# Attention residual: x plus the output's bias made in DRAM by accumulating DMAs instead of on GpSimd

## The chip, the cores and the metric

The kernel runs on one core of a Trainium2 chip. The metric is the device time of one execution in microseconds (us). The core has five engines that run their own instruction streams in order: TensorE (PE, matrix products; PEld is its weight load), VectorE (DVE), ScalarE (ACT), GpSimd (POOL) and SyncE (SP, which here only issues DMAs). 16 DMA engines move data between DRAM and the on-chip memory; SP, ACT and POOL each have a queue into them.

## The reference, cut to what matters

Four sequences of 1024 tokens, 512 channels, 16 heads of 32. First a cross attention on a layernorm of x, with a mask by token groups (768 image tokens in three chunks that see only their own chunk, then 256 text tokens that see all image tokens and, causally, text), then a feed-forward block with fake-quantised activations and weights. All of it is float32.

```python
def _L0_xattn_ref(q, kv, Wq, bq, Wk, bk, Wv, bv, Wo, bo, txt_tok_len, img_tok_len):
    ...
    attn = jax.nn.softmax(scores, axis=-1)
    out = jnp.einsum('bhqk,bhkd->bhqd', attn, vh)
    out = out.transpose(0, 2, 1, 3).reshape(B, N, C)
    return out @ Wo + bo

x = x + _L0_xattn_ref(_layernorm(x, axis=-1), ctx_1024, ...)
x = x + _L0_ffn_ref(_layernorm(x, axis=-1), ...)
```

The sum `x + out @ Wo + bo` is what the change is about. The kernel folds the bias of the values into it as well: since the softmax rows sum to one, `bv @ Wo + bo` is one row of 512 numbers that is added to every token. It is called the output's bias below.

## The kernel before, in words

**Blocks and units.** The 4096 tokens are cut into 16 query blocks of 256 tokens, numbered c = 0 to 15, four to a sequence: three image blocks and one text block. A unit is one block, one group of four heads (g = 0 to 3) and, for text, one block of keys (part 0 to 3). There are 112 units: for a sequence 12 of image blocks, then 16 of the text block (the last sequence has its text block second). Index n of the main loop counts units. In turn n the loop makes the scores of unit n (`s`, L446 or L457), their row maxima on DVE (L450, L468), the shifted scores and exponentials of unit n - 5 (`t` L504 and L509, `pT` L514 and L518) and the product with the values of unit n - 6 (`av` L554). The denominators are sums of the exponentials, made on POOL (`sp` L535) and folded by a product with ones (`av` L573); DVE takes the reciprocal (L588) and POOL multiplies (L589).

**What fills PE between them.** In each turn `large` takes one larger step: a part of the projection of a query, key or value block (`pp_q`, `pp_kv`, `pv`) or of the output projection of a finished block (`po`); all of these are recorded under L226. Jobs come in the order kv 0, q 0, kv 1, q 1 and so on, and a planner (`target`, `can_big`, `can_small`) sets in which turn each step falls. This plan depends on the indices alone, never on times.

**Layernorm of x.** For a coming query block, `next_queries` loads x into the tile `xb` (one buffer, L136 in `load_block`) and puts three functions into the queue `background`: `statistics` (DVE, L365), `deviation` (two ACT and seven small POOL instructions, L370 to L379: layernorm's factors) and `apply` (ACT L383, then the DMA `xn_d<-xb` of SP, L385, which frees `xb`). One function is taken from `background` in each turn; stages of the feed-forward weights' quantisation stand in the same queue. `load_spread` (L146) loads a kv block, or reads `xn_d` back, in the order that VectorE's 32x32 transposes need; `small_step` does that transpose (L267), one turn later at the earliest. In its turn the DVE instructions stand in a fixed order.

**The output of a block.** `Output.load` loads x for the block into `xr` (two buffers). `Output.add_bias` adds the output's bias `bo_b` on POOL (L613, one instruction of 128x1024 for a block), put off to a later turn by the list `later`. `Output.take` adds the product `po` to `xr` on DVE (L618), puts statistics for the second layernorm into `background`, and at the end stores the block into the DRAM tile `x1_d` by a DMA of POOL (L631). The feed-forward stage reads `x1_d` by L1019.

**The output's bias** is made in turns 2 to 5 by `spread`, `product` and `total` (DVE L206 writes `bo_b`).

**Order.** PE, DVE, ACT and POOL run in the order in which the program is written. SP's DMAs are put in order by the framework's scheduler, which moves a DMA forward to where its inputs and its buffer are ready: in the profile the first two `xr` loads are issued at 12.9 and 20.6 us though their blocks end much later. On the chip SP then issues in that fixed order and waits at each for what it needs.

Of the kernel before, what the change touches and what calls it, by code (L numbers as in the profile page):

```python
# [10 lines left out]
F32 = mybir.dt.float32  # L11
# [3 lines left out]
ALU = mybir.AluOpType  # L15
# [4 lines left out]
P = 128  # L20
B, N, C = 4, 1024, 512
NH, D = 16, 32
FF = 1408
NCC = C // P
NIC = FF // P
QB = 256
NQB = N // QB
# [15 lines left out]
def kernel(ctx: ExitStack, tc: tile.TileContext, x, kv, Wq, bq, Wk, bk, Wv, bv, Wo, bo, clip_x, clip_down, w_gate, w_up, w_down, out):  # L43
    nc = tc.nc
    x_tok = x.rearrange("b n c -> (b n) c")
# [5 lines left out]
    dram = ctx.enter_context(tc.tile_pool(name="dram", bufs=1, space=DRAM))  # L51

    x1_d = dram.tile([B * N, C], F32, tag="x1_d", name="x1_d")
    xn_d = [dram.tile([QB, C], F32, tag=f"xn_d{c}", name=f"xn_d{c}") for c in range(B * NQB)]
    h_d = [dram.tile([P, NIC, TB], F32, tag=f"h_d{i}", name=f"h_d{i}") for i in range(NTB - RESIDENT)]

# [65 lines left out]
    with ExitStack() as actx:  # L122
        wk2 = actx.enter_context(tc.tile_pool(name="wk2", bufs=2))
# [4 lines left out]
        ap = actx.enter_context(tc.tile_pool(name="ap", bufs=1))  # L128
# [5 lines left out]
        def load_block(src, c, tag, bufs=1):  # L134
            t = ld.tile([P, 2, C], F32, tag=tag, name=f"{tag}_{c}", bufs=bufs)
            nc.sync.dma_start(t, src[c * QB : (c + 1) * QB, :].rearrange("(t p) c -> p t c", p=P))  # L136
            return t
# [10 lines left out]

        brow = ap.tile([3 * NCC, P], F32, tag="brow", name="brow")
        bqk = ap.tile([P, 3 * NCC], F32, tag="bqk", name="bqk")  # L150
        bo_b = ap.tile([P, C], F32, tag="bo_b", name="bo_b")
        mask = ap.tile([P, P], F32, tag="mask", name="mask")
        NMB = 4
        nm2s = [ap.tile([P, 2, 4, D], BF16, tag=f"nm2_{i}", name=f"nm2_{i}") for i in range(NMB)]
# [18 lines left out]

        def other_loads():
            nc.sync.dma_start(W["Wo"], Wo.rearrange("(c p) f -> p c f", p=P))
            nc.gpsimd.dma_start(bo_b, bo.partition_broadcast(P))
            for name, clip in (("x", clip_x), ("h", clip_down)):
                sig[name] = cpool.tile([P, 1], F32, tag=f"sig_{name}", name=f"sig_{name}")
                nc.gpsimd.dma_start(sig[name], clip.partition_broadcast(P))
# [8 lines left out]
        def output_bias():  # L188

            bvr = wk2.tile([P, NCC, D], F32, tag="wst", name="bvr", bufs=1)  # L190
            parts = wk2.tile([P, C], F32, tag="sp", name="bo_parts")

            def spread():
                nc.vector.memset(bvr, 0.0)
                nc.vector.tensor_copy(bvr[:, :, 0:1], bqk[:, 2 * NCC :].unsqueeze(2))

            def product():
                pb = ps_sc.tile([P, 2, 2, QB], F32, tag="sc", name="pbo").rearrange("p a b c -> p a (b c)")[:, 0, :]
                for cc in range(NCC):
                    nc.tensor.matmul(pb[rows_of(cc)], bvr[:, cc, :], W["Wo"][:, cc, :], start=True, stop=True, tile_position=(0, cc * D), skip_group_check=True)  # L200
                nc.scalar.copy(parts, pb)

            def total():
                pb = ps_sc.tile([P, 2, 2, QB], F32, tag="sc", name="pbt").rearrange("p a b c -> p a (b c)")[:, 0, :]
                nc.tensor.matmul(pb, ones, parts, start=True, stop=True)
                nc.vector.tensor_tensor(bo_b, pb, bo_b, ALU.add)  # L206

            return spread, product, total

# [41 lines left out]
        class Job:  # L251


            def __init__(self, kind, c, a):
                self.kind, self.c, self.a = kind, c, a
                self.small, self.big, self.part = 0, 0, 0
                self.smalls = 2 if c == 0 else 1
                self.bigs = 4 if kind == "kv" else 2
# [93 lines left out]
        background = deque()  # L352
# [54 lines left out]
        def rows_of(j):  # L407
            return slice(j * D, (j + 1) * D)
# [181 lines left out]

                return avs, av, quotient

        at_end = [False]
        later = []

        class Output:


            def __init__(self, k):
                self.k, self.xr, self.i, self.part, self.biased = k, None, 0, 0, False  # L600

            def load(self):
                if self.xr is None:
                    self.xr = load_block(x_tok, self.k.c, "xr", bufs=2)
                    if at_end[0]:
                        later.append(self.add_bias)
                    else:
                        later.append(lambda: later.append(self.add_bias))

            def add_bias(self):  # L610
                if not self.biased:
                    self.biased = True
                    nc.gpsimd.tensor_tensor(self.xr, self.xr, bo_b.unsqueeze(1).to_broadcast([P, 2, C]), ALU.add)  # L613

            def take(self, po, i, cols):
                self.add_bias()
                xr, t0 = self.xr, 2 * self.k.c
                nc.vector.tensor_tensor(xr[:, i, cols], po[:, cols], xr[:, i, cols], ALU.add)  # L618
                if cols.stop < C:
                    return None  # L620
                name = f"st2_{self.k.n}_{i}"

                def statistics():
                    st = small.tile([P, 6], F32, tag="st2", name=name)
                    nc.vector.bn_stats(st, xr[:, i, :])
                    nc.vector.bn_aggr(mv2[:, t0 + i, :], st)
                    nc.vector.tensor_reduce(xm2[:, t0 + i, 0:1], xr[:, i, :], AX.X, ALU.max)
                    nc.vector.tensor_reduce(xm2[:, t0 + i, 1:2], xr[:, i, :], AX.X, ALU.min)

                if i == 1:  # L630
                    nc.gpsimd.dma_start(x1_d[t0 * P : (t0 + 2) * P, :].rearrange("(t p) c -> p t c", p=P), xr)  # L631
                return statistics
# [50 lines left out]
        T_LAG, V_LAG = 5, 6  # L683
        units = []
        for b in range(B):
            for qb in range(NQB) if b < B - 1 else (0, TEXT, 1, 2):
                k = Block(b, qb)
# [3 lines left out]
        LATE = len(units) - n_text - 3 * NCC  # L691
# [94 lines left out]
        def step_output(half=False, rests=False):  # L786
            rest = outputs[0].step(half)
            if outputs[0].i == 2:
                outputs.pop(0)

                def take():
                    rest[1]()
                    for o in outputs[:2]:
                        o.load()

                finish((rest[0], take), rests)
            else:
                finish(rest, rests)
# [57 lines left out]
        stage()  # L856
        stage()
        take()
        spent, rows_done["k", 0] = 2 * BIG, NCC
        stage()  # L860
# [9 lines left out]
        send(3)  # L870
        big_step()
        other_loads()
        early[0] = False
        spread, product, total = output_bias()
        for n in range(len(units) + V_LAG):
            at_end[0] = n >= len(units)
            previous = units[n - 1] if 0 < n <= len(units) else None
            if n < len(units):
                u = units[n]
# [6 lines left out]
                    minus_maxima(u)  # L886
            if n in (2, 3, 4, 5):
                (spread, sigmoids, product, total)[n - 2]()
            f = background.popleft() if background and n > 0 else None
            if f is not None and f.__name__ in ("deviation", "apply", "quantise"):  # L890
                f()
                f = background.popleft() if background and f.__name__ == "quantise" else None
# [100 lines left out]
        for i in range(2):  # L993
            t = t0 + i
# [27 lines left out]
    gctx = ExitStack()  # L1022
    f4 = gctx.enter_context(tc.tile_pool(name="f4", bufs=NTT))
    fd = gctx.enter_context(tc.tile_pool(name="fd", bufs=1))
    fd.tile([P, 56], F32, tag="pad", name="pad")

    fx = gctx.enter_context(tc.tile_pool(name="fx", bufs=2))
    xt = load_x1(fx, 0)
# [160 lines left out]
    def steps(h):  # L1189

        return h.rearrange("p i t -> p (i t)").bitcast(BF16).rearrange("p (i u) -> p i u", i=NIC)[:, :, :TB]
# [9 lines left out]
    for n, tb in enumerate(order):  # L1201
        hq, xr = steps(resident[tb]), xrs.pop(tb)
# [74 lines left out]
```

## Time and profile before

| | |
|---|---|
| time, median of 3 runs | 1131.82 us (1130.69 to 1134.02) |
| the profiled execution | 1132.25 us, span 1130.5 us |
| TensorE clock granted | 0.995 of full speed |
| PE busy | 1106.8 us, 98% of the span |
| DVE, ACT, POOL busy | 783.8, 502.1, 549.0 us |
| POOL L613 (the bias) | 16 instructions, 38.1 us |
| POOL L535 (the sums) | 143 instructions, 328.4 us |
| DMA moved | 119.09 MB, mean 105 GB/s |

The attention stage lasts to about 872 us, the feed-forward stage from there. Idle time of PE in the profile is time between the modelled end of one product and the start of the next; PEld's idle time is the gap in the weight loads, of which some 0.3 us stand at many changes of operation without a loss.

### The profile page before, as it was taken

The numbers are of one execution on the slowest core, as the hardware profiler recorded it, in microseconds if no ns is written. First come the engines' busy times: TensorE is split into PE (matmuls) and PEld (weight loads), VectorE is DVE, ScalarE is ACT, GpSimd is POOL, SyncE is SP. The second block draws the span as 40 slices with busy tenths as digits, with TensorE's granted clock in tenths as the row PEclk, the third lists the DMA queues.
The fourth block names the chain that finished last, engine by engine and source line by source line (L and its number), as shares of the span: only waits on it lengthen the run. The fifth ranks groups of instructions, "written<-read, shape, count | busy, mean of one in ns | idle before, by whom it ended". The sixth has DMA issues, their size and how long they took to land.

```text
span 1130.5 us, 31464 instructions
## 1 busy us (share of the span) xinstructions
PE 1106.8 (98%) x13829; PEld 553.5 (49%) x13851; DVE 783.8 (69%) x980; ACT 502.1 (44%) x701; POOL 549.0 (49%) x616
## 2 busy tenths in 40 slices
PE   9999999999999999999999999999999899998998
PEld 5545545454445445454544445555544344443444
DVE  2546676766577857567777656876666788877887
ACT  3234444343444434344433345544342465553553
POOL 1224556677754576775646668668753232110110
PEclk9999999999999999999999999999999899999999
DMA  8342223132322231331323123112221599311895
GB/s 261 111 132 65 63 56 96 47 97 76 90 63 76 74 97 43 94 104 36 89 66 88 41 74 86 42 50 63 73 76 47 185 289 253 73 34 33 299 379 191
DMA packets 117201, 119.09 MB, mean 105 GB/s; under 512 B 55548, under 2 KB 86536, under 8 KB 115656
## 3 DMA queue, kind: packets, MB, share of 16 engines
q1 hardware_dynamic: 111104, 83.26, 26.7%
q0 software_dynamic: 5648, 33.30, 7.8%
q8 instruction: 108, 1.77, 0.7%
q10 hardware_dynamic: 312, 0.53, 0.2%
q14 instruction: 29, 0.24, 0.1%
HBM read 71.57 MB, written 33.29 MB: 93 GB/s over the span
## 4 chain that ended last, share of the span: by engine, by line
PE 84%; POOL 7%; DVE 3%; DMA 3%; ACT 2%; issue 1%; POOLq 0%; DVEq 0%; SPq 0%; ACTq 0%
PE pv L226 9%; PE pp_kv L226 8%; PE pp_q L226 8%; PE av L554 8%; PE po L226 8%; PE t L509 7%; PE pg L1117 7%; PE pu L1117 7%; PE s L457 5%; POOL sp L535 4%; PE s L446 4%; PE av L573 3%; PE t L504 3%; PE pd L1220 2%; DMA xt<-x_d 2%
## 5 line engine op out<-in xcount | busy, mean ns | idle before, releaser
L514 ACT ACTIVATE pT<-t 128x1024 f32<-128x1024 f32 x112 | 114.8, 1025 | 332.1 <-PE t L509 310.0
L535 POOL TENSOR_TENSOR sp<-sp,pT 128x1024 f32<-128x1024 f32 x84 | 188.2, 2240 | 45.0 <-ACT pT L518 41.6
L535 POOL TENSOR_TENSOR sp<-pT 128x1024 f32<-128x1024 f32 x59 | 140.2, 2376 | 97.7 <-ACT pT L518 86.7
L468 DVE TENSOR_REDUCE nmh<-s 128x2 f32<-128x1024 f32 (+1 forms) x128 | 145.2, 1157 | 60.1 <-PE s L457 57.9
L450 DVE TENSOR_REDUCE nmh<-s 128x4 f32<-128x1024 f32 x96 | 112.8, 1218 | 84.3 <-PE s L446 84.3
L226 PE MATMUL pv<-Wv_sb,kvT 128*32 128x512 f32 (+1 forms) x1088 | 120.5, 570 | 1.6 <-DVE xr L618 1.6
L226 PE MATMUL pp_q<-qT,Wq_sb 128*32 128x256 f32 x2048 | 121.3, 380 | 0.2
L554 PE MATMUL av<-pT,va 128*32 128x256 f32 (+1 forms) x1792 | 116.9, 377 | 0.0
L226 PE MATMUL po<-Wo_sb,oT 128*32 128x512 f32 (+1 forms) x1120 | 112.2, 534 | 2.7 <-DVE xr L618 2.4
L518 ACT ACTIVATE pT<-t 128x1024 f32<-128x1024 f32 x112 | 114.5, 1023 | 0.0
L509 PE MATMUL t<-qT,kT 32*128 32x256 f32 (+1 forms) x1792 | 113.4, 366 | 0.0
L226 PE MATMUL pp_kv<-kvT,Wk_sb 128*32 128x256 f32 x1920 | 112.5, 380 | 0.1
L588 DVE RECIPROCAL avs<-avs 128x256 f32<-128x256 f32 x63 | 109.7, 1742 | 0.0
L509 PEld LDWEIGHTS t<-qT,kT 32*128 32x128 f32 x1792 | 88.1, 184 | 6.7
L1117 PE MATMUL pg<-xqT,wgT 128*128 128x512 bf16 x344 | 90.0, 381 | 1.1 <-DVE xqT L1078 0.5
L1117 PE MATMUL pu<-xqT,wuT 128*128 128x512 bf16 x345 | 90.2, 382 | 0.4
L589 POOL TENSOR_TENSOR oT<-avs 128x256 f32<-128x256 f32 x63 | 46.2, 734 | 90.1 <-DVE avs L588 89.9
L1123 ACT ACTIVATE silu<-pg,sg 128x512 f32<-128x512 f32 x88 | 60.0, 687 | 65.3 <-PE pg L1117 63.2
L226 PEld LDWEIGHTS pp_q<-qT,Wq_sb 128*32 128x32 f32 x2048 | 63.3, 110 | 48.3 <-issue 5.5
L1144 DVE SCALAR_TENSOR_TENSOR h<-pu,su,silu 128x512 f32<-128x512 f32 x88 | 65.4, 747 | 30.5 <-PE pu L1117 27.8
L226 PEld LDWEIGHTS pp_kv<-kvT,Wk_sb 128*32 128x32 f32 x1920 | 60.2, 110 | 43.6 <-issue 2.3
L554 PEld LDWEIGHTS av<-pT,va 128*32 128x32 f32 x1792 | 47.0, 109 | 53.5 <-issue 30.0
(191 smaller groups left out, 1448.0 us busy)
## 6 DMA issues: line engine op xcount, KB each, us to landing
xt<-x_d SPq DMA_DIRECT2D x16, 1024.0 KB, 6.1
h<-h_d POOLq DMA_DIRECT2D x3, 2816.0 KB, 14.2
xb<-in_x_dram SPq DMA_DIRECT2D x16, 512.0 KB, 3.7
xr<-in_x_dram SPq DMA_DIRECT2D x16, 512.0 KB, 3.6
x_d<-xr POOLq DMA_DIRECT2D x16, 512.0 KB, 3.7
spread_kv<-in_ctx_dram SPq DMA_DIRECT2D x60, 128.0 KB, 2.8
xn_d<-xb SPq DMA_DIRECT2D x15, 512.0 KB, 3.4
spread_q<-xn_d SPq DMA_DIRECT2D x60, 128.0 KB, 2.7
```

The costliest lines, as they stand in the source:

```text
L226: nc.tensor.matmul(out[rows_of(j)], lhs[:, rows_of(j)], rhs, start=start, stop=stop, tile_position=(0, j * D), skip_group_check=True)
L450: nc.vector.tensor_reduce(nmh[:, h, :, :, 0], prs[h], AX.X, ALU.max, negate=True)
L468: nc.vector.tensor_reduce(nmh[:, h, :, i, half], s[:, :, :n], AX.X, ALU.max, negate=True)
L509: nc.tensor.matmul(prs[j // 2][:, j % 2, n, cols], kc[rows_of(j), g, n * P : (n + 1) * P], q[rows_of(j), g, cols], start=False, stop=(n == 1))
L514: nc.scalar.activation(pT[:, :2], prs[0], AF.Exp)
L518: nc.scalar.activation(pT[:, 2:], prs[1], AF.Exp)
L535: nc.gpsimd.tensor_tensor(sp[:, :, cols], a, pT[:, :, n, cols], ALU.add)
L554: nc.tensor.matmul(av[rows_of(j), 0, cols], va[:, n, g * P + j * D : g * P + (j + 1) * D], u.pT[:, j, n, cols], start=(u.part == 0 and n = ...
L588: nc.vector.reciprocal(avs[:, 1, :], avs[:, 1, :])
L1117: nc.tensor.matmul(ps, w[:, cc, ic * P : (ic + 1) * P], qT[:, cc, :], start=(cc == 0), stop=(cc == NCC - 1))
L1123: nc.scalar.activation(s, pg, AF.Silu, scale=sg[:, ic : ic + 1])
L1144: nc.vector.scalar_tensor_tensor(h[:, ic, :], pu, su[:, ic : ic + 1], s, ALU.mult, ALU.mult)
```

## The change

Five things are changed.

1. After `total`, SP writes the row `bo_b[:1]` into a DRAM tile `bo_d`, and four DMAs of SP (one for a sequence, 2 MB each) fill all of `x1_d` with copies of that row.
2. In turns n = 7 to 22 a DMA of POOL adds x of block c = n - 7 to those rows of `x1_d` (`accum_op=ALU.add`, DRAM to DRAM, rows of 2 KB).
3. `Output.load` reads `x1_d` instead of x; `add_bias` and its POOL instruction are gone. `xr` has three buffers instead of two.
4. In turns up to LATE in which the exponentials are those of a text unit of part 2 or 3, nothing is taken from `background` if `deviation` is next in it.
5. `bo_b` takes one of the three `oT` buffers instead of its own, and is loaded by SP instead of POOL; a pad in the feed-forward stage grows by 2 KB.

```diff
+    bo_d = dram.tile([1, C], F32, tag="bo_d", name="bo_d")
...
-        bo_b = ap.tile([P, C], F32, tag="bo_b", name="bo_b")
+        bo_b = wk2.tile([P, NCC, QB], F32, tag="oT", name="bo_b", bufs=3).rearrange("p a b -> p (a b)")[:, :C]
...
-            nc.gpsimd.dma_start(bo_b, bo.partition_broadcast(P))
+            nc.sync.dma_start(bo_b, bo.partition_broadcast(P))
...
                 nc.vector.tensor_tensor(bo_b, pb, bo_b, ALU.add)
+                nc.sync.dma_start(bo_d, bo_b[:1, :])
+                for b in range(B):
+                    nc.sync.dma_start(x1_d[b * N : (b + 1) * N, :], bo_d.to_broadcast([N, C]))
...
             def load(self):
                 if self.xr is None:
-                    self.xr = load_block(x_tok, self.k.c, "xr", bufs=2)
-                    if at_end[0]:
-                        later.append(self.add_bias)
-                    else:
-                        later.append(lambda: later.append(self.add_bias))
-
-            def add_bias(self):
-                if not self.biased:
-                    self.biased = True
-                    nc.gpsimd.tensor_tensor(self.xr, self.xr, bo_b.unsqueeze(1).to_broadcast([P, 2, C]), ALU.add)
+                    self.xr = load_block(x1_d, self.k.c, "xr", bufs=3)
 
             def take(self, po, i, cols):
-                self.add_bias()
...
             if n in (2, 3, 4, 5):
                 (spread, sigmoids, product, total)[n - 2]()
-            f = background.popleft() if background and n > 0 else None
+            if 7 <= n < 7 + B * NQB:
+                rows = slice((n - 7) * QB, (n - 6) * QB)
+                nc.gpsimd.dma_start(x1_d[rows, :], x_tok[rows, :], accum_op=ALU.add, max_dma_last_dim=C)
+            t = units[n - T_LAG] if T_LAG <= n < LATE else None
+            crowded = t is not None and t.k.text and t.part > 1
+            f = background.popleft() if background and n > 0 and not (crowded and background[0].__name__ == "deviation") else None
...
-    fd.tile([P, 56], F32, tag="pad", name="pad")
+    fd.tile([P, 568], F32, tag="pad", name="pad")
```

More of the change, by code (lines that the diff above doesn't have):

```diff
@@ L591, in values @@
                 return avs, av, quotient
-        at_end = [False]
         later = []
@@ L599, in __init__ @@
             def __init__(self, k):
-                self.k, self.xr, self.i, self.part, self.biased = k, None, 0, 0, False
+                self.k, self.xr, self.i, self.part = k, None, 0, 0
             def load(self):
                 if self.xr is None:
-                    self.xr = load_block(x_tok, self.k.c, "xr", bufs=2)
-                    if at_end[0]:
-                        later.append(self.add_bias)
-                    else:
-                        later.append(lambda: later.append(self.add_bias))
-            def add_bias(self):
-                if not self.biased:
-                    self.biased = True
-                    nc.gpsimd.tensor_tensor(self.xr, self.xr, bo_b.unsqueeze(1).to_broadcast([P, 2, C]), ALU.add)
+                    self.xr = load_block(x1_d, self.k.c, "xr", bufs=3)
             def take(self, po, i, cols):
-                self.add_bias()
                 xr, t0 = self.xr, 2 * self.k.c
@@ L875 @@
         for n in range(len(units) + V_LAG):
-            at_end[0] = n >= len(units)
             previous = units[n - 1] if 0 < n <= len(units) else None
```

## The prediction

> **What bounds the kernel now.** I read the shares of busy time first. PE is the bound, and what any change of another engine can give is limited to PE's holes.
>
> ```profile
> PE 1106.8 (98%) x13829; PEld 553.5 (49%) x13851; DVE 783.8 (69%) x980; ACT 502.1 (44%) x701; POOL 549.0 (49%) x616
> ```
>
> Next I listed what PE waited for between 20 and 865 us, the attention stage (engine, line, releaser: us in total, times, longest).
>
> ```profile
> PE av L573 <- POOL sp L535: 2.6, 7, 0.7
> PE po L226 <- DVE xr L618: 2.4, 2, 1.8
> PE pv L226 <- DVE xr L618: 1.6, 2, 0.8
> ```
>
> The releaser `DVE xr L618` stands behind POOL's bias instruction: the list of all waits has DVE waiting 18.0 us, in 4 cases, for `POOL xr L613`. PE's timeline gives the single holes (start, duration, instruction, idle time before it).
>
> ```profile
> 291.70 0.64 PE L573 MATMUL av<-sp,ones 128*32 128x256 f32 x8 [0.71 <-POOL sp L535]
> 308.75 2.78 PE L226 MATMUL pv<-Wv_sb,kvT 128*32 128x512 f32 x24 [0.78 <-DVE xr L618]
> ...
> 858.96 3.64 PE L226 MATMUL po<-Wo_sb,oT 128*32 128x512 f32 x32 [1.80 <-DVE xr L618]
> ```
>
> The hole at 291.70 follows a `deviation` that POOL ran from 284.99 to 286.79, ahead of the last part's sums; its twin is at 504.62. The holes at 308.75, 521.67, 840.49 and 858.96 are the bias. So L613's 38.1 us are nearly all idle time of POOL put to use; only these holes cost anything.
>
> **What is removed.** Bias: PE's holes sum to 0.78 + 0.78 + 0.58 + 1.80 = 3.9 us; by the gaps of the weight load (1.18, 1.18, 1.06 and 2.28 us, less 0.33 that such a change of operation shows anyway) 4.4. Without L613 the instruction L618 starts when `po` is done, and with a third `xr` buffer the load that came at 852 us is issued before it is needed. Factors: 0.71 + 0.71 = 1.4 us, by the weight loads 2 x (1.19 - 0.33) = 1.7; the other five holes before L573 follow ScalarE's late exponential or the weights' cast and the store L631, which stay. A `deviation` kept back by up to two turns moves `xn_d` back by as much; its block is projected more than a turn after its spread load, so I cost this at nothing, with half a turn (3.5 us) if that cover is gone. Gain: 5.4 to 6.1 us, I take 5.8.
>
> **What POOL gets.** 16 accumulating DMAs in turns 7 to 22. Storing 512 KB in 2 KB rows (L631) occupies POOL 0.81 us; an accumulate has a second read, so at most twice that: 13 to 26 us against 38 removed. Between 70 and 180 us POOL is busy 54 of 110 us, so nothing of it reaches PE; without the cover, one of the later ones ahead of a text part's sums would cost one hole of 0.8 us. Behind each waits POOL's own stream, the sums and `nm`. The first needs sequence 0's 2 MB filled; by the working below it is full at about 83 us, and POOL reaches turn 7's DMA at about 88. The third `xr` buffer, `bo_b` in an `oT` buffer (free again long before the third block asks for it), the pad, and `bo_b` on SP's queue at the start have one answer: no time.
>
> **What SP's queue gets.** This decides. The four filling DMAs are 8.39 MB in SP's queue, which also carries every load that DVE needs. Here is SP in these turns, then DVE:
>
> ```profile
> 71.39 1.52 SPq L492 DMA_TRANSPOSE nmT<-nm  x1
> 75.57 0.38 SPq L385 DMA_DIRECT2D xn_d<-xb  x1
> 78.37 0.39 SPq L136 DMA_DIRECT2D xb<-in_x_dram  x1
> 78.86 1.17 SPq L492 DMA_TRANSPOSE nmT<-nm  x1
> 80.21 1.93 SPq L146 DMA_DIRECT2D spread_q<-xn_d  x4
> ```
> ```profile
> 87.51 1.74 DVE L588 RECIPROCAL avs<-avs 128x256 f32<-128x256 f32 x1
> 89.17 0.64 DVE L365 BATCH_NORM_STATS2 st<-xb 128x6 f32<-128x512 f32 x1
> ...
> 90.99 2.15 DVE L267 STREAM_TRANSPOSE qT<-spread_q 128x1024 f32<-128x1024 f32 x1 [0.17 <-PE pp_q L226]
> 93.08 2.31 DVE L450 TENSOR_REDUCE nmh<-s 128x4 f32<-128x1024 f32 x2
> ```
>
> Does a small load wait behind a large one in this queue? At the start it does. The usual landing of a spread load of 128 KB is in the list of DMA issues; the four that are issued at 7.58 us, behind 2 MB of `Wv` and `Wq`, have this instead (second line, least, median and most):
>
> ```profile
> spread_kv<-in_ctx_dram SPq DMA_DIRECT2D x60, 128.0 KB, 2.8
> DMA to landing us min/median/max: 9.8/10.0/10.2
> ```
>
> An `xr` load of 512 KB behind `Wo` took 12.1 us against 3.6. So the queue serves in order.
>
> Now the times. `total` (L206) ends at 70.18 + 0.67 = 70.85. The write of `bo_d`: 0.4 to issue and about 2 to land (the smallest store of this trace, 128 KB of the output, lands in 1.7), so the fills are issued at about 73.2 and their first packets run at 74.1 (`xn_d`'s came 0.9 after its issue). How long 8.39 MB take no row shows, since nothing here goes from DRAM to DRAM. Fast end: loads of 2 KB rows at full load.
>
> ```profile
> 20.00:25.00 5.00, 5.00 (x62) 1.98 (x64) 1.17 (x1) 1.35 (x3) 0.00 (x0) 1.00 0.96 352
> ```
>
> The last column is GB/s: 8.39 MB / 352 = 23.8 us. Slow end: the only read of one row by all engines, `bo_b`'s load, whose packet records show a median of 279 ns for 4 KB against 160 for a store L631: 2048 packets / 16 engines x 279 ns = 35.7 us. The fill does both, reads one row and writes DRAM; I take the middle, 30. The fills then end at 104 (98 to 110).
>
> The Trainium skill's page "DMA: Bandwidth & Descriptors", section "Anatomy of one DMA — SWDGE (gpsimd) path", fits a DMA by 2.0 us plus its bytes over 436 GB/s. No run here shows that rate, and the trace's best is the 352 GB/s above. By it the fills would last 21.2 us as an estimate, and the stall worked out next would be some 9 us shorter, the net some +2.
>
> `xn_d` is ready at 75.57 and finds the fills in the queue: its 512 KB land at about 104 + 1.5 + 1 = 106.5. `xb` may only be loaded when `xn_d` has been read, and lands 2.8 later, 109.4. DVE's statistics (89.17 now) thus wait 20.2 us (14 to 26), and everything behind them in DVE's order: the transpose L267, then turn 8's maxima. PE cannot go on without those: the second pair of `t` in turn 8 (about 96.05) takes the PSUM buffer whose maxima end at 94.25, the third buffer of three. Slack 1.8 us, stall 18.4 us (12.4 to 24.2). If SP's order puts `xn_d` ahead of the fills, `xb` comes directly behind them, at 106.5: stall 15.5 (9.5 to 21.5). I take 17. Loads and transposes behind that have 10 to 28 us of slack in their turns and are late only with PE. POOL's `sp` and ACT are idle meanwhile and catch up, so the loss is paid once.
>
> Sum: 1132.25 + 17 - 5.8 = 1143.4 for an execution like the profiled one; this lies 0.4 above the median, so 1143.0. The case's own range: +9.5 - 6.1 = +3.4 to +24.2 - 5.4 = +18.8, that is 1135 to 1151.
>
> **The rivals.** *Hidden fills, faster.* The fills don't hold up `xn_d` and `xb`, because the scheduler puts them behind these loads, or because a copy from DRAM to DRAM leaves the engines gaps which the other packets take. For it: the DMA engines are busy 0.41 of the time between 75 and 90 us, so there is room, and nobody needs `x1_d` before the first block's output near 142 us. Against it: the landings at the start. Price: only the gain, 1131.8 - 5.8 = 1126.0. It decides once `xb` lands before 91 us (89.17 plus the slack).
> *Between.* Fills at the fast end, with `xn_d` sent before them: a stall of 3 to 9 us against 5.8 of gain, 1129 to 1135. The measurement can tell about 0.3% (3.4 us) from no change, so half of this case is "same".
> *Slow fills.* If reading one row holds at the rate of `bo_b`'s whole load (256 KB from first to last packet in 1.73 us, 150 GB/s), the fills last 56 us, POOL's first accumulate waits too, and PE stalls some 43 us: 1169.
> *The change doesn't do what it says:* rule 4 would be idle if no `deviation` met parts 2 or 3; those at 285 and 498 us did, and it is worth 1.4 us at most.
>
> **How the numbers follow.** Queue stall as worked out 0.58; slow fills 0.07; between 0.13; hidden 0.22. Slower by over 0.3%: 0.58 + 0.07 + 0.04 = 0.69; same: 0.09; faster: 0.22. The range takes in the hidden case's 1126 with half a us below it, and ends at 1152; out of it are the slow fills and a little more.
>
> **What would show it.** Right: in the profile after, one PE hole of 9 to 24 us near 96 us with DVE's L365 waiting for the DMA of `xb`; landings over 20 us for `xn_d` or `xb`; DMA share near 1 from 74 to 104; no holes before L226 from L618; the holes at 291 and 504 gone; POOL's accumulates about 0.8 to 1.6 us each. Wrong: `xb` landing in a few us beside the fills, or fills that are spread thin, or a new hole at the text groups' ends from late factors.

## The result and the profile after

The changed kernel takes 1192.14 us (median of 5 runs, 1189.4 to 1193.88) against 1131.82: 1.0529 times as long, with a 95% interval of 1.0508 to 1.0549. It is slower, as forecast, but by 60 us where 11 were forecast, and far outside the range. The profiled execution has a span of 1190.4 us and a mean granted clock of 0.968.

First the page's shares of busy time, then its 40 slices of 29.8 us, digits in tenths.

```profile
PE 1112.1 (93%) x13851; PEld 555.5 (47%) x13851; DVE 783.8 (66%) x980; ACT 502.0 (42%) x701; POOL 531.7 (45%) x615
...
PE   9993069999999999999999999999999899999898
...
PEclk9996579999999999999999999999999899999999
DMA  6369978794322223123222312212321289510795
GB/s 222 110 121 128 125 156 150 137 159 80 99 77 60 73 68 103 55 80 84 66 56 91 84 39 69 78 45 64 109 54 57 97 245 302 130 28 9 274 382 199
```

All of the damage lies in slices 4 to 6 (89 to 179 us): PE falls to 3, 0 and 6 tenths and its clock to 6, 5 and 7. The DMA row shows 9 in slices 4 and 5, yet the row below it only 128 and 125 GB/s: full engines that move little.

What PE waited for most between 20 and 865 us, and PE's timeline at the ends of the two holes:

```profile
PE t L508 <- DVE nmh L454: 56.1, 1, 56.1
PE av L558 <- issue: 4.5, 1, 4.5
PE av L577 <- POOL sp L539: 1.7, 7, 0.3
```
```profile
94.12 1.50 PE L558 MATMUL av<-pT,va 128*32 128x256 f32 x12 [4.55 <-issue]
...
159.80 0.61 PE L508 MATMUL t<-nmT,onesb 2*128 2x512 bf16 x2 [56.13 <-DVE nmh L454]
```

One hole is nearly the whole loss. The groups `po` and `pv` behind L618 are gone from the list, and the waits for the sums (`sp`) fell from 2.6 to 1.7 us: the gain is there too. Now SP, which issues the loads, and DVE, which needs them:

```profile
70.57 0.29 SPq L208 DMA_DIRECT2D bo_d<-bo_b  x1
71.89 29.14 SPq L210 DMA_DIRECT2D x_d<-bo_d  x4
101.15 22.40 SPq L496 DMA_TRANSPOSE nmT<-nm  x1
123.64 9.00 SPq L389 DMA_DIRECT2D xn_d<-xb  x1
149.51 0.40 SPq L137 DMA_DIRECT2D xb<-in_x_dram  x1
```
```profile
87.26 1.74 DVE L592 RECIPROCAL avs<-avs 128x256 f32<-128x256 f32 x1
153.37 0.69 DVE L369 BATCH_NORM_STATS2 st<-xb 128x6 f32<-128x512 f32 x1 [64.37 <-DMA xb<-in_x_dram]
...
156.65 1.99 DVE L271 STREAM_TRANSPOSE qT<-spread_q 128x1024 f32<-128x1024 f32 x1 [1.58 <-DMA spread_q<-xn_d]
158.56 2.31 DVE L454 TENSOR_REDUCE nmh<-s 128x4 f32<-128x1024 f32 x2
```

This is the chain of the prediction, link by link. SP sits in the four fills for 29 us and in one transposing DMA behind them for 22. `xn_d` goes out at 123.64 and lands 25.8 us later; only then is `xb` loaded; DVE's statistics wait 64 us for it, and the maxima that PE's hole names come last, at 158.56. The list of DMA issues (KB each, median us to landing) and the view of the fills' line (L210) give the fill's own time, and the windows (length; busy time and count of PE, PEld, DVE, ACT, POOL; granted clock; DMA share; GB/s) its rate:

```profile
x_d<-bo_d SPq DMA_DIRECT2D x4, 2048.0 KB, 52.9
```
```profile
DMA to landing us min/median/max: 39.3/52.9/66.4
```
```profile
74.00:148.00 74.00, 25.12 (x348) 12.74 (x347) 8.35 (x6) 8.39 (x13) 10.14 (x9) 0.67 1.00 123
...
159.80:164.80 5.00, 5.00 (x50) 2.94 (x53) 2.74 (x2) 1.94 (x2) 3.29 (x11) 0.53 0.68 139
```

The fills' first packet stands at 73.2 us. The last fill is issued at 81.45 and lands 66.4 us later, at 147.8: 8.39 MB in 74.6 us, 112 GB/s, with the engines' share at 1.00. The 2 KB packets have a median of 191 ns and a mean of 262 ns. Below, too, the time of the fills is taken from the first packet to the landing of the last fill.

### The profile page after: what moved, and what is told of

It reads as the page before. It is cut to its first block, busy times and chain, and to the rows that moved or that the text cites. A ratio compares the mean times of both kernels' runs of the same rounds, so it can differ in the third digit from the quotient of the medians.

```text
span 1190.4 us, 31499 instructions
## 1 busy us (share of the span) xinstructions
PE 1112.1 (93%) x13851; PEld 555.5 (47%) x13851; DVE 783.8 (66%) x980; ACT 502.0 (42%) x701; POOL 531.7 (45%) x615
## 4 chain that ended last, share of the span: by engine, by line
PE 79%; DMA 8%; POOL 4%; DVE 3%; SPq 2%; ACT 2%; issue 2%; ACTq 0%; POOLq 0%; DVEq 0%
PE po L230 8%; PE pv L230 8%; PE av L558 8%; PE pp_q L230 8%; PE pp_kv L230 7%; PE t L513 7%; PE pg L1114 7%; PE pu L1114 6%; PE s L461 5%; PE s L450 3%; POOL sp L539 3%; PE av L577 3%; PE t L508 3%; DMA xn_d<-xb 2%; PE pd L1217 2%; SPq L496 2%
## 5 line engine op out<-in xcount | busy, mean ns | idle before, releaser
L508 PE MATMUL t<-nmT,onesb 2*128 2x512 bf16 x448 | 46.4, 385 | 56.3 <-DVE nmh L454 56.1
L1120 ACT ACTIVATE silu<-pg,sg 128x512 f32<-128x512 f32 x88 | 60.0, 686 | 64.9 <-PE pg L1114 64.9
```

The costliest lines, as they stand in the source:

```text
L508: nc.tensor.matmul(prs[j // 2][:, j % 2, :, :], onesb[j * D : j * D + 2, :], rhs, start=True, stop=False)
```

## The experiments

Theory: DVE waits for loads that the fills hold up, and the fills last 75 us because 16 engines read the same 2 KB row of DRAM. Rivals: a copy from DRAM to DRAM is that slow whatever it reads; 8 MB are too much however read; the order of SP's queue does it, so that another queue would spare the loads. Line numbers in the profiles are those of each kernel, a few lower or higher than in the changed one. Diffs are against the changed kernel where nothing else is said; three dots mark lines that are left out.

### The source of the fill

**e1_fill_from_sbuf** reads the bias from the 128 partitions of `bo_b` on the chip, each of which holds the row.

```diff
-    bo_d = dram.tile([1, C], F32, tag="bo_d", name="bo_d")
...
-                nc.sync.dma_start(bo_d, bo_b[:1, :])
...
-                    nc.sync.dma_start(x1_d[b * N : (b + 1) * N, :], bo_d.to_broadcast([N, C]))
+                    nc.sync.dma_start(x1_d[b * N : (b + 1) * N, :].rearrange("(t p) c -> p t c", p=P), bo_b.unsqueeze(1).to_broadcast([P, N // P, C]))
```

> The four fills stay where they are, on SP's queue in turn 5, and write the same 8.39 MB, but read the row from bo_b in on-chip memory (all 128 partitions hold it) instead of bo_d in DRAM. Theory (the fills are slow because 16 DMA engines read one DRAM row at once; the queue then holds up xn_d and xb): packets of 2 KB come back to 84-100 ns from a median of 192 and the fills last 22-28 us instead of some 75; xb lands near 103-109 us instead of 153, the hole of PE is 12-18 us instead of 56, the time 1138-1146. Rival A (the volume written to DRAM is what takes the time, whatever is read): fills of 70 us or more, a hole of 50 us or more, 1183-1195. Rival B (not the fills but the accumulating DMAs or the third xr buffer make the loss): no change, 1189-1194.

Measured: 1142.79 us, ratio 1.0098 (1.0082 to 1.0115). Its PE hole, its fills and the window over them:

```profile
111.18 0.61 PE L506 MATMUL t<-nmT,onesb 2*128 2x512 bf16 x2 [14.66 <-DVE nmh L452]
```
```profile
x_d<-bo_b SPq DMA_DIRECT2D x4, 2048.0 KB, 18.7
```
```profile
74.00:96.00 22.00, 22.00 (x352) 11.55 (x346) 8.47 (x6) 8.82 (x14) 10.18 (x9) 1.00 1.04 366
```

The same bytes to the same place, again with the engines full, but at three times the rate: they run from 72.7 us to a last landing at 97.6, 24.9 us or 337 GB/s, with a packet median of 87 ns. The hole is the same wait, 41 us shorter, and it ends 48.6 us earlier; the time falls by 49.3. The volume alone leaves a hole of some 15 us; the rest of the loss belongs to the source.

**e2_fill_distinct_rows** keeps DRAM to DRAM and reads a different row of x for each row written.

```diff
-                    nc.sync.dma_start(x1_d[b * N : (b + 1) * N, :], bo_d.to_broadcast([N, C]))
+                    dst, src = (r[b * N : (b + 1) * N, :].rearrange("(p t) c -> p t c", t=2) for r in (x1_d, x_tok))
+                    for t in range(2):
+                        nc.sync.dma_start(dst[:, t, :], src[:, 1 - t, :])
```

> The fills read distinct rows of 2 KB of x from DRAM (odd rows into even places and the reverse, eight DMAs of 1 MB on SP's queue at the same place) instead of one row; the attention's residual is then x plus a swapped x without the bias. Theory (one row read by all engines is slow): 22-30 us of fills, a hole of 12-20 us, 1138-1148. Rival C (a copy from DRAM to DRAM is slow by itself, whatever its rows): packets stay near 190 ns, fills 65-80 us, 1180-1195.

Measured: 1146.5 us, ratio 1.0128 (1.0112 to 1.0145). These copies need nothing that is computed, so SP's order put them at 20.6 us, and the hole came at 61.75:

```profile
20.59 20.08 SPq L212 DMA_DIRECT2D x_d<-in_x_dram  x8
```
```profile
61.75 2.08 PE L452 MATMUL s<-kT,qT 32*128 32x256 f32 x12 [17.58 <-DVE nmh L456]
```

As a test of place it fails; as a test of rate it stands: the copies last from 20.6 to 53.1 us, 258 GB/s beside other loads of the kernel's start, packet median 84 ns. A copy from DRAM to DRAM isn't slow in itself.

**f3_fill_128_rows** and **g3_fill_16_rows** keep the broadcast from DRAM, with more copies of the row in `bo_d`: 128 and 16. f3's edit is below; g3 has 16 for P in all of it.

```diff
-    bo_d = dram.tile([1, C], F32, tag="bo_d", name="bo_d")
+    bo_d = dram.tile([P, C], F32, tag="bo_d", name="bo_d")
...
-                nc.sync.dma_start(bo_d, bo_b[:1, :])
+                nc.sync.dma_start(bo_d, bo_b)
...
-                    nc.sync.dma_start(x1_d[b * N : (b + 1) * N, :], bo_d.to_broadcast([N, C]))
+                    nc.sync.dma_start(x1_d[b * N : (b + 1) * N, :].rearrange("(t p) c -> p t c", p=P), bo_d.unsqueeze(1).to_broadcast([P, N // P, C]))
```

> As the change, from DRAM to DRAM on SP's queue in turn 5, but bo_d has 128 rows with the same contents (256 KB), and the copies read all of them. Theory (the same 2 KB read by 16 engines is what is slow; equal contents at 128 places are not): fills of 22-32 us, packets of 84-110 ns, a hole of PE of 13-22 us, 1140-1150. Rival (a broadcast of bo_d, or a copy from DRAM to DRAM at this place, is slow however many rows it has): 190 ns, 1180-1195.

> As f3, but bo_d has 16 rows instead of 128, one for each DMA engine's share of a fill. Theory (many engines on one row are what is slow): as f3, fills of 25-32 us, a hole of 18-26 us, 1147-1156. Rival F (a row that is read again and again is slow even for one engine, or 32 KB lie too close together): fills of 40 us or more, a hole of 30 us or more, over 1165.

Measured: 1151.21 us, 1.0173 (1.0159 to 1.0187), and 1154.43 us, 1.0205 (1.0182 to 1.0228). First f3's hole and fills, then g3's hole:

```profile
118.38 0.61 PE L508 MATMUL t<-nmT,onesb 2*128 2x512 bf16 x2 [21.92 <-DVE nmh L454]
```
```profile
x_d<-bo_d SPq DMA_DIRECT2D x4, 2048.0 KB, 22.0
```
```profile
123.70 0.61 PE L508 MATMUL t<-nmT,onesb 2*128 2x512 bf16 x2 [26.94 <-DVE nmh L454]
```

Still DRAM to DRAM, still each row read many times: f3's fills last 31.0 us (271 GB/s) and g3's 35.4 (237 GB/s). From one row to 16 the fill becomes 2.1 times as fast, and 128 rows take off another 4.4 us. f3's time lies 1.2 us above its range; g3's fills and hole are a little longer than expected (25 to 32 and 18 to 26 us). In the four kernels that issue the fills from SP in turn 5, PE goes on 12.0 to 13.6 us after the last fill has landed:

| | last fill lands, us | PE goes on, us |
|---|---|---|
| e1 | 97.6 | 111.2 |
| f3 | 106.3 | 118.4 |
| g3 | 110.9 | 123.7 |
| changed kernel | 147.8 | 159.8 |

So the theory holds: it is the single row that all engines read, and the hole follows the end of the fills. What in the memory makes that slow, these runs don't tell. One difference remains: e1, f3 and g3 also write the rows in another order than the changed kernel. In e2 each copy writes every second row in turn, which is nearly the old order, and it is fast too, so the order is an unlikely reason; no run changes it alone.

### The queue

**e4_fill_by_pool_queue** leaves the one row and lets POOL issue the fills; **g1_sbuf_pool_queue** does the same to e1.

```diff
-                    nc.sync.dma_start(x1_d[b * N : (b + 1) * N, :], bo_d.to_broadcast([N, C]))
+                    nc.gpsimd.dma_start(x1_d[b * N : (b + 1) * N, :], bo_d.to_broadcast([N, C]))
```

> As the change, bo_d as source, but the four fills are issued by POOL, so that they stand in POOL's queue and not in SP's. Theory (order in SP's queue holds up xn_d and xb): these two now share the engines with the slow fills instead of waiting for their end; xn_d and xb land in 4-12 us each, the hole near 96 us shrinks to 0-15 us, the first accumulates wait on POOL for the fills as before; 1126-1150. Rival E (the engines are busy with slow packets, and any load suffers whatever its queue): a hole of 40 us or more, 1175-1195.

> As e1 (four fills of 2 MB in turn 5 that read bo_b in on-chip memory at full rate), but issued by POOL, so they stand in POOL's queue and not in SP's. It tells apart the order in SP's queue from the load on the 16 engines, with fills that last some 25 us. Theory (SP's loads wait because they stand behind the fills in one queue): xn_d and xb share the engines with the fills, land in 5 to 9 us each, the hole near 96 us is 0-6 us, 1124-1132. Rival E (the engines are full, and a load waits in whichever queue it stands, as e4 hints): a hole of 10-17 us, 1137-1146.

Measured: 1187.6 us, 1.0496 (1.048 to 1.0512), and 1143.5 us, 1.0107 (1.0091 to 1.0122). SP's timeline of e4, then DVE's:

```profile
79.21 0.40 SPq L389 DMA_DIRECT2D xn_d<-xb  x1
101.26 0.39 SPq L137 DMA_DIRECT2D xb<-in_x_dram  x1
...
105.84 11.52 SPq L147 DMA_DIRECT2D spread_q<-xn_d  x4
```
```profile
122.97 0.69 DVE L369 BATCH_NORM_STATS2 st<-xb 128x6 f32<-128x512 f32 x1 [33.65 <-DMA xb<-in_x_dram]
...
151.16 1.98 DVE L271 STREAM_TRANSPOSE qT<-spread_q 128x1024 f32<-128x1024 f32 x1 [26.49 <-DMA spread_q<-xn_d]
```

SP is free now, and sends `xn_d` at 79.21, 44 us earlier. Its data also land before the fills end (about 101 us), so it does pass them. But it takes 22 us where 3.3 are usual, `xb` nearly another 22, and then `spread_q` keeps DVE for 26. Three transfers, each of which needs the one before or stands behind it in DVE's order, crawl one after another, and PE's hole is 51.5 us instead of 56.1. That is the rival's case, and the theory of the expectation (a hole of 0 to 15 us) fails. With the fast source the two queues differ by less: hole 15.7 in g1, 14.7 in e1. The edit changes one thing more: in the trace the fills that POOL issues go out in packets of 4 KB (median 390 ns in e4, 173 in g1), SP's in packets of 2 KB. The fills last about as long (73.5 us in e4, 26.8 in g1); what packets of 2 KB in POOL's queue would do to the loads is not tested.

The Trainium skill's page "DMA: Bandwidth & Descriptors", section "Queues, rings and completion order", says that each DMA engine goes round between the queues that have work and takes a whole packet, typically some 9 to 17 descriptors, from one before it turns to the next. e4 agrees in that the transfers get through; it shows as well that a turn in the round is little help beside the slow fills. Whether a packet of the profile is one of the page's, no run here shows. In both runs the first packet comes late (`xn_d` 10 us after its issue in e4, 6 in g1); what that wait is made of is open.

### Spreading the fills

**e3_spread_sbuf_pool** issues eight fills of 1 MB from the on-chip `bo_b` by POOL, in turns 6 to 13, and starts the accumulates one turn later. SP's four fills and `bo_d` are gone.

```diff
-                nc.sync.dma_start(bo_d, bo_b[:1, :])
-                for b in range(B):
-                    nc.sync.dma_start(x1_d[b * N : (b + 1) * N, :], bo_d.to_broadcast([N, C]))
...
+            if 6 <= n < 6 + B * NQB // 2:
+                rows = slice((n - 6) * 2 * QB, (n - 5) * 2 * QB)
+                nc.gpsimd.dma_start(x1_d[rows, :].rearrange("(t p) c -> p t c", p=P), bo_b.unsqueeze(1).to_broadcast([P, 4, C]))
-            if 7 <= n < 7 + B * NQB:
-                rows = slice((n - 7) * QB, (n - 6) * QB)
+            if 8 <= n < 8 + B * NQB:
+                rows = slice((n - 8) * QB, (n - 7) * QB)
```

> The fills are cut into eight of 1 MB, read bo_b in on-chip memory, and are issued by POOL in turns 6 to 13, one in a turn; the accumulating DMAs follow in turns 8 to 23. Theory (the loss is only the queue that is held up in one place, and the gain of the holes at the bias and the factors is real): 1 MB in 3-4 us of each turn of 7 us holds up no load of DVE by more than its slack, PE has no hole over 1 us between 70 and 200 us, the time is 1124-1129, before less 4 to 8. Rival D (the other DMAs of the change cost too: 16 accumulates at 1.35 us of POOL, 25 MB of extra traffic): 1131-1140, with holes of PE spread over turns 6 to 23.

Measured: 1135.06 us, 1.0024 (1.0012 to 1.0036). The 1124 to 1129 of the theory are missed; the time lies in rival D's range, but without the spread of holes that D has. One hole is left, at turn 12:

```profile
134.16 1.99 DVE L267 STREAM_TRANSPOSE qT<-spread_q 128x1024 f32<-128x1024 f32 x1 [7.60 <-DMA spread_q<-xn_d]
```
```profile
137.31 0.61 PE L504 MATMUL t<-nmT,onesb 2*128 2x512 bf16 x2 [5.59 <-DVE nmh L468]
```

Here `spread_q` lands in up to 11.3 us, while 1 MB of fill and 512 KB of accumulate go out in each turn beside it. Thinner still is **f2_paced**: one 512 KB fill by POOL in each even turn from 6, from 128 rows, and its accumulate in the turn after, in 2 KB packets (512 B in the changed kernel and e3), so that all of it spreads over 32 turns. `bo_d` is made as in f3, and SP's four fills are gone.

```diff
-            if 7 <= n < 7 + B * NQB:
-                rows = slice((n - 7) * QB, (n - 6) * QB)
-                nc.gpsimd.dma_start(x1_d[rows, :], x_tok[rows, :], accum_op=ALU.add, max_dma_last_dim=C)
+            if 6 <= n < 6 + 2 * B * NQB:
+                rows = slice((n - 6) // 2 * QB, ((n - 6) // 2 + 1) * QB)
+                if n % 2 == 0:
+                    nc.gpsimd.dma_start(x1_d[rows, :].rearrange("(t p) c -> p t c", p=P), bo_d.unsqueeze(1).to_broadcast([P, 2, C]))
+                else:
+                    nc.gpsimd.dma_start(x1_d[rows, :], x_tok[rows, :], accum_op=ALU.add, max_dma_last_dim=4 * C)
```

> bo_d with 128 rows; POOL fills one block of 512 KB in every even turn from 6 and adds x to it in the next turn (with packets of 2 KB instead of 512 B), up to turn 37. At most one transfer of 0.5 to 1.5 MB stands in a turn of 7 us. Theory (the loss is only the burst that holds up SP's loads): no hole over 1 us, the time of f5 plus at most 1 us: 1125-1127.5, faster than before. Rival D (the accumulates cost in themselves, by the wait of SP's xr loads or POOL's 1.3 us each): 1128-1135, with holes between 75 and 300 us.

Measured: 1125.87 us, 0.9945 (0.9931 to 0.9958). This version beats both kernels, the one before by half a per cent. PE's longest wait between 20 and 865 us, the DMA issues, and the first part of their turns as a window:

```profile
PE av L575 <- POOL sp L537: 2.4, 7, 1.0
```
```profile
x_d<-bo_d POOLq DMA_DIRECT2D x16, 512.0 KB, 4.5
x_d<-in_x_dram POOLq DMA_DIRECT2D x16, 512.0 KB, 6.4
```
```profile
70.00:180.00 110.00, 109.31 (x1648) 55.84 (x1644) 74.80 (x78) 48.19 (x75) 59.27 (x80) 1.00 0.66 150
```

The DMA engines have 0.66 of their time filled, and PE is busy for 109.31 of 110 us. f2 differs from e3 in the source and in the accumulates' packets too. **g4_paced_one_row** asks whether the pace would do with the slow source: f2 with the one-row `bo_d` of the changed kernel. Its diff is against f2.

```diff
-                    nc.gpsimd.dma_start(x1_d[rows, :].rearrange("(t p) c -> p t c", p=P), bo_d.unsqueeze(1).to_broadcast([P, 2, C]))
+                    nc.gpsimd.dma_start(x1_d[rows, :], bo_d.to_broadcast([QB, C]))
```

> As f2 (one block filled in every even turn, x added in the next), but bo_d is one row again, so each fill of 512 KB is read at the slow rate and lasts some 4.7 us of two turns (14 us). Theory (the slow row costs only where its burst outlasts the slack of DVE's loads): a hole of 0-6 us in all, 1125-1132. Rival (while one row is read by all engines, every load beside it is held up): several holes of 2-5 us, 1135-1160.

Measured: 1127.76 us, 0.9965 (0.9953 to 0.9978); a fill lands in 6.4 us instead of 4.5, and the longest hole before the sums is 0.82 us. So the pace does nearly all of it, even with the slow source. What the accumulates' larger packets have of it isn't separated.

### The gain

**f5_no_bias** is the changed kernel without fills and accumulates; `xr` is loaded from x, so the output's bias is left out. **f1_factors_only** is the kernel before with the fourth point of the change alone.

```diff
-                nc.sync.dma_start(bo_d, bo_b[:1, :])
-                for b in range(B):
-                    nc.sync.dma_start(x1_d[b * N : (b + 1) * N, :], bo_d.to_broadcast([N, C]))
...
-                    self.xr = load_block(x1_d, self.k.c, "xr", bufs=3)
+                    self.xr = load_block(x_tok, self.k.c, "xr", bufs=3)
...
-            if 7 <= n < 7 + B * NQB:
-                rows = slice((n - 7) * QB, (n - 6) * QB)
-                nc.gpsimd.dma_start(x1_d[rows, :], x_tok[rows, :], accum_op=ALU.add, max_dma_last_dim=C)
```
```diff
-            f = background.popleft() if background and n > 0 else None
+            t = units[n - T_LAG] if T_LAG <= n < LATE else None
+            crowded = t is not None and t.k.text and t.part > 1
+            f = background.popleft() if background and n > 0 and not (crowded and background[0].__name__ == "deviation") else None
```

> The kernel after without the fills and the accumulating DMAs; xr is loaded from x with three buffers, so the output's bias is left out. It shows what the change can win at most. Theory (the gain is the holes at the bias and the factors, 5.4 to 6.1 us, a little more with the shrunk ones): 1124.5-1126.5, no hole of PE over 0.5 us between 100 and 865 us. Rival (holes that are removed come back elsewhere): 1128-1132.

> The kernel before with part 4 of the change alone (deviation kept out of turns with the exponentials of a text unit's parts 2 and 3). Theory: the holes before L573 at 291.7 and 504.6 go (2 x 0.71 us, 0.86 by the weight loads) and those at 235.5 and 448.4 shrink, as they do in the profile after: 1.4 to 2.3 us less, 1129.2-1130.2. Rival: the factors that come later hold up a projection and it is given back: 1131-1133.

Measured: f5 1125.57 us, 0.9943 (0.993 to 0.9955); f1 1132.14 us, 0.9995 (0.9985 to 1.0004). PE's timeline in f1, once at the place of the factors and once at that of the bias:

```profile
291.98 0.64 PE L573 MATMUL av<-sp,ones 128*32 128x256 f32 x8 [0.21 <-POOL sp L535]
...
858.63 3.64 PE L226 MATMUL po<-Wo_sb,oT 128*32 128x512 f32 x32 [1.78 <-DVE xr L618]
```

f5 shows what the change is worth if its transfers cost nothing: 6.2 us. f1 missed its expectation: the factors' holes shrink from 0.71 to 0.21 us, 1.0 us for both, but not to nothing, and the time doesn't show it. The holes at the bias are still there (1.78 us), as they have to be.

## Why the prediction was wrong

**Right: which chain decides.** The direction, the wait (DVE's statistics for `xb`, then the transpose, then turn 8's maxima and the second pair of `t`) and its being paid once are as written. Where the fills had nearly the duration that the prediction gave them, so had the rest: e1's lasted 24.9 us, near the fast end (23.8), and its hole of 14.7 us lies between the 9.5 and 24.2 of the stall. From the end of the fills to PE's going on the prediction has 10.4 us (104 to 114.4), the table above 12.0 to 13.6. That e1's 1142.79 us stand beside the predicted 1143.0 is luck: its stall is shorter than the 17 of the sum, and the half clock, which the sum doesn't have, makes up for part of it.

**Right: the gain.** "I take 5.8" against 6.2 in f5 and 5.9 in f2. Its division was off: the factors gave 1.0 us in place of 1.4 to 1.7. The holes that are gone from PE's list in f5 (`po` 2.4, `pv` 1.6, `sp` 2.6 to 1.8) make 4.8 of the 6.2; where the rest comes from isn't shown.

**Wrong, and nearly all of the error: how long 8.39 MB take.** The step reads: "2048 packets / 16 engines x 279 ns = 35.7 us", taken as the slow end, and "I take the middle, 30". It was 74.6 us. The row for it had been found, `bo_b`'s load as "the only read of one row by all engines", but two rates of it stood in the text, and the wrong one was used. The median duration of a packet (4 KB in 279 ns) leaves out the long packets and the time between them. The rate over the whole load, 150 GB/s or 56 us, was put into a rival with 0.07, and it was misread: in the trace the load's 64 packets stand from 31.63 to 33.78 us, 2.15 us and not 1.73, which is 122 GB/s. By that the fills would last 69 us, within a tenth of what they did at 112 GB/s. The fills' own records show the same trap: at their median of 191 ns, 4096 packets on 16 engines would be 49 us. With 74.6 us of fills the second pair of `t` starts at 159.8 instead of 96.05 us, 63.8 us later where the sum has 17. The fit of the Trainium skill's page "DMA: Bandwidth & Descriptors", section "Anatomy of one DMA — SWDGE (gpsimd) path", gave 21.2 us as an estimate. That falls somewhat short of e1's 24.9; for the one row the measurement decides, 3.5 times as long. (That 352 GB/s were "the trace's best" is a misreading too: the 40 slices of the profile before reach 379. The sum doesn't hang on it.)

**Wrong: "So the queue serves in order" as the reason.** It describes SP in the changed kernel, but isn't what the loss hangs on: e4 and g1 take the fills out of that queue and keep the hole. Here full engines delay a transfer from another queue too (`xn_d` 22 us in e4, 12.6 in g1, against 3.3). The start of the kernel, on which the step rested, couldn't tell the two apart, since there both the queue and the engines were full (DMA share 1.04 from 7 to 18 us).

**Not in the sum.** The span after exceeds that of f5 (1125.5) by 64.9 us. The second pair of `t`, at which PE waits, stands in f5 among these four products:

```profile
96.66 0.40 PE L504 MATMUL t<-nmT,onesb 2*128 2x512 bf16 x4
```

It starts there at 96.66 us and in the changed kernel at 159.80: 63.1 us by that place. The other 1.8 us lie behind it, where PE runs at half clock, as the window from 159.8 us shows (0.53). The smaller hole, of 4.5 us, which ends at 94.12 with "issue" as its cause, is no term of its own: it and the half clock behind it only bring PE to the big wait later, at 103.7 us, and that wait ends when `xb` lets it. So the hole reads 56.1 us where the stall is some 63. The smaller one stands only where the fills are slowest (here and, with 3.75 us, in e4). In the kernel before, a 16 KB packet of an instruction queue (q8, which I take for PE's) stands at 82.6 us; in these two at 91.9 and 91.4, just ahead of that hole's end, and in e1, f3, g3 and g1, which have no such hole, at 85 to 86. That late instructions are the cause is argued from this, not shown.

**POOL.** An accumulate occupies it for 1.35 us, inside "0.81 to 1.6":

```profile
L883 POOL DMA_DIRECT2D x_d<-in_x_dram x16 | 21.6, 1349 | 4.4 <-DMA x_d<-bo_d 4.1 <-issue 0.3
```

The wait that the prediction ruled out (sequence 0 full "at about 83 us") did come, 4.1 us, since its fill took till 92; it is small beside the hole.

**The rivals.** *Hidden fills* isn't what this change does, but the paced versions are that case, at 1125.9 where it said 1126.0. *Slow fills* had the mechanism and fell short, 1169 against 1192: 56 us of fill for 74.6 and 43 of stall for some 63, and no half clock behind it.

## What to carry to other kernels

Price a transfer by its bytes over the time from first to last packet of the row most like it, not by the median of its packets, and read that time off the records with care; keep a row that reads memory in the same odd way (here one row by all engines) as the value and not as the far end. A constant that is to be spread over DRAM is read from the chip or from several copies. Bulk DMA that nobody waits for is cut into pieces and issued over many turns: it is the load on the engines that delays small loads which somebody does wait for, and another queue doesn't cure that.

## What the runs showed of the hardware that was not expected

**One row read by 16 engines** is copied at 112 GB/s; 16 rows at 237, 128 rows at 271, all different rows at 258 (beside the loads of the start), and rows from the chip at 337 GB/s, all written to DRAM in 2 KB packets from SP's queue. In g3 two of the 16 engines finish the last fill some 4 us behind the others.

**PE's clock after a wait.** In the first 2 us after e3's hole of 5.6 us the granted clock is 0.50, as after the hole of 56:

```profile
137.30:139.30 2.00, 1.99 (x18) 1.59 (x17) 2.00 (x2) 0.00 (x0) 0.00 (x0) 0.50 1.05 400
139.30:141.30 2.00, 2.00 (x24) 0.83 (x24) 0.74 (x1) 1.02 (x1) 0.73 (x1) 0.50 1.26 226
141.30:143.30 2.00, 2.00 (x40) 1.18 (x36) 0.00 (x0) 1.20 (x3) 0.00 (x0) 0.93 1.31 201
```

It is back about 4 us after the hole's end here, and 3.3 (g1) to 6.1 us (g3) after it in the other runs. The Trainium skill's page "TensorE: Matmul & The Clock Gate", section "🔬 Part 1: The HAM clock gate (the "warmup" mystery)", gives the array two states, half and full clock, which change after an idle or a busy window of some 3.4 us. The runs agree with the half; back at full clock they are later than one such window in all but g1. Such a hole thus cost somewhat more than itself: e3's span exceeds f5's by 7.0 us with a hole of 5.6, and from the product behind the hole to the end e1, f3, g3, g1, e4 and the changed kernel take 0.0 (g1) to 3.2 us (g3) longer than f5 from the same product.

**A small transfer beside a bulk one** (`xn_d`, 512 KB) took 22 us in e4 and 12.6 in g1, against 3.3, though it had a queue of its own.
